# Linear attention: the products with the carried sum and the product of k and v issued as 32-column products, in one step with the products of the values

## Chip, core and metric

The kernel runs on one core of one Trainium2 chip. The metric is the device time of one execution in microseconds (us); the time before is the median of three executions. TensorE executes the matrix products, VectorE (DVE), ScalarE (ACT) and GpSimd (POOL) the elementwise work, and SyncE (SP) issues the DMA transfers. In the profile, PE is the row of matrix products of TensorE and PEld the row of its weight loads.

## What is computed

The program is a stack of four blocks over an input of 8 sequences, 1024 positions and 256 features, all in float32, each block with a layer norm in front and a residual around it: linear (flow) attention with its own feed-forward, a dense feed-forward, softmax attention, and a feed-forward with 4-bit quantized operands. The change lies in the first one:

```
q = sigmoid(heads(Wq)); k = sigmoid(heads(Wk)); v = heads(Wv)       # 16 heads of 16
...
vs = v * src_comp[..., None]
kv = cumsum(einsum('bhld,bhlm->bhldm', k, vs), axis=2)              # causal, per head 16 x 16
x  = einsum('bhld,bhldm->bhlm', qs, kv) * sink_alloc[..., None]
attn = x @ Wo + bo
```

The kernel computes the causal sum in chunks of 128 positions. For each chunk it adds two parts: the product of q with the sum of k times v over all earlier chunks of the sequence (the carried sum, called `kv_sum`), and the masked products of q and k inside the chunk times the values of the chunk.

## The kernel before

A sequence has 8 chunks of 128 positions, in two groups of four, so there are 64 chunks and 16 groups. A planner (class `Plan`) writes the program out: every piece of work is a generator that yields what it needs next (tiles, PSUM banks, a free slot), the planner keeps for each engine a modelled time at which it is free, and the part that can go first goes next (`run`, line 231). `took` (line 140) holds the modelled costs; for a matrix product it takes a quarter of the cost where the weights have at most 32 columns (line 158). All five engines are kept in exactly the order in which the instructions were issued (`PINNED`, line 38), and every instruction is issued through one helper, so that the profile shows one line, L268, for all of them and groups have to be told apart by the names of tiles. Since the order follows from the modelled costs and from the needs, an edit of one part moves the work of all others too.

The parts that run side by side are the linear attention (`linear_group`, `linear_chunk`), the two dense feed-forwards (`dense`, with `norms_1` and `norms_2`) and softmax attention with the quantized feed-forward (`soft_chunk`). PSUM has 8 banks, and a part asks for as many as it needs with `banks=`.

A chunk of linear attention (`linear_chunk`, line 897) goes through these steps:

- `bank<-wqkv,n0T` makes the values; DVE adds the bias and writes the scaled values into a padded tile `v_pad` (5 buffers), where each head has 32 columns, half of them zero.
- ACT writes `qz`, q split by even and odd heads, and TensorE makes the products of q and k in four groups of 32 rows (`bank<-qz,k`, line 951). DVE masks them into four tiles `sc` (line 963).
- TensorE turns k round (`bank<-ident,k`, line 973) and ACT copies it to SBUF as `kT`.
- The output bank: two products of full width with the carried sum (`bank<-q,kv_sum`, lines 980 to 990) and 16 products whose weights have 32 columns (`bank<-sc,v_pad`, lines 991 to 1001), all accumulated in the same bank. ACT copies the bank to `xo`.
- After that, as a need of its own that the planner may place later (line 1006): two products of full width of `kT` with the values (`bank<-v_pad,k`, lines 1008 to 1015). DVE multiplies them with the block diagonal `bdiag`, so that only the 16 x 16 block of each head stays (`kv`, line 1018), and POOL adds them to the carried sum (`kv_sum`, line 1028). The last chunk of a sequence leaves this step out, and the first one has no carried sum, so each is done 56 times.
- `bank<-w_L_attn_Wo,xo` is the output projection of the chunk.

The two products of k and v before:

```
yield pe(kT, banks=1)
kvbank = mm_bank()
for k in range(2):
    nc.tensor.matmul(kvbank[:, k * P : (k + 1) * P], lhsT=kT[:, k, :],
                     rhs=v_columns(pad, range(4 * k, 4 * k + 4)), start=True, stop=True)
```

`v_columns(pad, pairs)` (line 652) picks the nonzero columns of the given pairs of heads, 32 columns for a pair.

Of the kernel before, what the change touches and what calls it, by code (L numbers as in the profile page):

```python
# [13 lines left out]
ALU = mybir.AluOpType  # L14
AX = mybir.AxisListType

P = 128
D = 256
# [39 lines left out]
class Plan:  # L58
# [142 lines left out]
    def pe(self, *tiles, **kw):  # L201
        return self.need("tensor", tiles, **kw)

    def dve(self, *tiles, **kw):
        return self.need("vector", tiles, **kw)

    def act(self, *tiles, **kw):
        return self.need("scalar", tiles, **kw)
# [78 lines left out]
def block_stack_kernel(ctx: ExitStack, tc: tile.TileContext, a: dict, out: bass.AP):  # L287
# [20 lines left out]
    plan = Plan(tc, tc.nc)  # L308
    nc, pe, dve, act, dma = plan, plan.pe, plan.dve, plan.act, plan.dma
# [15 lines left out]
    def mm_bank():  # L325
        bank = ps.tile([P, 512], F32, tag="bank", name="bank")
        plan.bank(bank)
        return bank
# [4 lines left out]
    def fresh(kind, need, name=None):  # L333

        need.fresh = kind
        yield need
        return make(kind, name)

    def make(kind, name=None):
        bufs, width, dtype = TILES[kind]  # L340
        t = wk.tile([P, width], dtype, tag=kind, name=name or kind, bufs=bufs)
        plan.take(kind, t)
        return t
# [29 lines left out]
    bdiag = const.tile([P, P], F32, name="bdiag")  # L373
# [130 lines left out]
    def turned(srcs):  # L504

        bank = tr_bank()
        for i, src in enumerate(srcs):
            nc.tensor.transpose(bank[:, i, :], src, ident)
        return bank[:, : len(srcs), :]
# [4 lines left out]
    def two(t):  # L514
        return t.rearrange("p (k t) -> p k t", k=2)
# [136 lines left out]
    def v_columns(v, pairs):  # L652

        return bass.AP(
            tensor=v.tensor,
            offset=v.offset + 64 * pairs.start,
            ap=[list(v.ap[0]), [64, len(pairs)], [64 - DH, 2], [1, DH]],
        )
# [38 lines left out]
    def running(out, cur, carry, b, first, last):  # L697
# [16 lines left out]
    count = {  # L714
        "halves": 0,
        "dense": 0,
        "acc": 0,
        "res": 0,
        "v": 0,
        "scored": 0,  # L720
        "attended": 0,
        "linear": 0,
# [14 lines left out]
    def half_fits(p, kind, half):  # L737
        return half in groups[p][kind] or count["halves"] < HALVES
# [11 lines left out]
    def linear_group(p):  # L750
# [143 lines left out]
        for i in range(G):  # L894
            plan.start(linear_chunk(p, i, n0T, comp, qk), p + 0.55 + 0.03 * i)

    def linear_chunk(p, i, n0T, comp, qk):

        s, g = divmod(p, NG)
        past, c = seqs[s]["past"], p * G + i  # L900
        here = slice(i * P, (i + 1) * P)
        yield pe(n0T, banks=1, when=lambda: count["v"] == c and c - count["attended"] < V_PADS)
        bank = mm_bank()
        for k in range(2):
            nc.tensor.matmul(
                bank[:, :D],
                lhsT=n0T[:, k, here],
                rhs=wqkv[:, k, 2 * D :],
                start=k == 0,
                stop=k == 1,  # L910
            )
        count["v"] += 1
        pad = v_pads[c % V_PADS]
# [17 lines left out]
                when=lambda: groups[p].get("scaled")  # L931
# [13 lines left out]
        banks = []  # L945
        for r in range(4):
            rows = slice(32 * r, 32 * r + 32)
            bank = mm_bank()
            banks.append(bank)
            for k in range(2):  # L950
                nc.tensor.matmul(
                    bank[:, k * D : (k + 1) * D],
                    lhsT=qk[1][rows, k, here],
                    rhs=qz[rows, k, :, :],
                    start=True,
                    stop=True,
                )
        plan.drop(tile_qz)
        scores = []
# [10 lines left out]
        end = g == NG - 1 and i == G - 1  # L970
        if not end:
            yield pe(banks=1, at=p + 0.66 + 0.06 * i, when=lambda: count["attended"] == c)
            bank = turned([qk[1][:, k, here] for k in range(2)])
            kT = two((yield from fresh("lin", act(bank), "k")))
            nc.scalar.copy(kT, bank)
        kv = past.get("kv")
        yield pe(pad, *scores, *([] if kv is None else [kv]), banks=1, when=lambda: count["attended"] == c)
        kv = past.get("kv")

        bank = mm_bank()[:, :D]  # L980
        for k in range(2):
            if kv is not None:
                nc.tensor.matmul(
                    bank[:, k * P : (k + 1) * P],
                    lhsT=kv[:, k, :],
                    rhs=qk[0][:, k, here],
                    start=k == 0,
                    stop=False,
                    skip_group_check=True,
                )  # L990
        for k in range(2):
            for e in range(2):
                for r in range(4):
                    nc.tensor.matmul(
                        bank[32 * r : 32 * r + 32, k * P : (k + 1) * P],
                        lhsT=pad[:, 8 * k + 2 * r + e, :],
                        rhs=scores[r][:, 2 * k + e, :],
                        start=kv is None and k == 0 and e == 0,
                        stop=k == 1 and e == 1,
                        skip_group_check=True,  # L1000
                    )
        plan.drop(*scores)
        xo = two((yield from fresh("lin", act(bank), "xo")))
        nc.scalar.copy(xo, two(bank))
        if not end:
            yield pe(kT, banks=1)
            kvbank = mm_bank()
            for k in range(2):
                nc.tensor.matmul(
                    kvbank[:, k * P : (k + 1) * P],  # L1010
                    lhsT=kT[:, k, :],
                    rhs=v_columns(pad, range(4 * k, 4 * k + 4)),
                    start=True,
                    stop=True,
                )
            plan.drop(kT)
            new = two((yield from fresh("lin", dve(kvbank), "kv")))
            nc.vector.tensor_tensor(
                new,
                two(kvbank[:, :D]),  # L1020
                bdiag.unsqueeze(1).to_broadcast([P, 2, P]),
                ALU.mult,
            )
            total = past["kv"] = wk.tile([P, 2, P], F32, tag="kv_sum", name="kv_sum", bufs=2)
            if kv is None:
                nc.gpsimd.tensor_copy(total, new)
            else:
                nc.gpsimd.tensor_tensor(total, kv, new, ALU.add)
            plan.drop(new)
        count["attended"] += 1  # L1030
        yield pe(xo, banks=1, at=p + 0.7 + 0.06 * i)
        bank = mm_bank()
        for k in range(2):
# [12 lines left out]
            banks=1,  # L1046
            at=p + 0.74 + 0.06 * i,
            when=lambda: half_fits(p, "hT", i // 2) and count["dense"] >= p - 1,
# [358 lines left out]
```

## Time and profile before

| quantity | value |
| --- | --- |
| median of three executions | 2785.93 us (2783.41 to 2787.86) |
| the profiled execution, its own time | 2781.91 us |
| its span, from the first to the last instruction | 2780.2 us |
| mean granted clock of TensorE | 0.983 |
| PE busy | 2643.3 us, 95% |
| DVE busy | 1947.2 us, 70% |
| ACT busy | 1255.4 us, 45%, of it 402.9 us in 314 table loads |
| POOL busy | 557.4 us, 20% |

A float32 matrix product leaves two records on the PE row and two on the PEld row: the 112 products with the carried sum appear as x224. Records overlap, since the next one starts before the one before it has ended, so the length of a record (275 ns at the median of these 224) is not what it costs; the distance between the starts of two groups is. A form such as `128*32 128x128` gives the rows and columns of the weights and then the size of the moving operand. The numbers in front of the lines of a timeline are the start and the length of a group in microseconds.

### The profile page before, as it was taken

What the parts mean: (1) busy time and instruction counts of PE and PEld (TensorE: products, weight loads), DVE (VectorE), ACT (ScalarE), POOL (GpSimd) and SP (SyncE); (2) the same over time, 40 slices, a digit from 0 to 9 for tenths busy, and PEclk for the clock granted to TensorE, in tenths of its full rate; (3) what the DMA queues carried; (4) which work ended last, traced back from release to release, by engine and by line L of the source; (5) the groups of instructions that cost most, each with busy time, mean ns of one, the idle gap of its engine ahead of it and who ended that gap; (6) DMA issues with size and microseconds to landing.
All of it is one profiled execution on the core that took longest, in us unless ns stands there. A gap on an engine that the chain in (4) does not pass through costs nothing.

```text
span 2780.2 us, 42805 instructions
## 1 busy us (share of the span) xinstructions
PE 2643.3 (95%) x15276; PEld 2018.2 (73%) x15276; DVE 1947.2 (70%) x4403; ACT 1255.4 (45%) x2482; POOL 557.4 (20%) x1100
## 2 busy tenths in 40 slices
PE   3978999999999999999999999999999999999997
PEld 1767777777777777777777777777777777777665
DVE  6877686785867768586685867668586766846565
ACT  2424443545444463545535454354544445444242
POOL 1323222121221212122131222212122121211000
PEclk7989999999999999999999999999999999999998
DMA  3234231322323222231222323132232312222000
GB/s 106 79 95 132 79 101 61 92 65 73 97 63 95 69 74 73 80 103 59 82 70 75 93 73 93 52 99 65 72 92 67 100 57 83 70 72 84 19 12 14
DMA packets 283204, 211.43 MB, mean 76 GB/s; under 512 B 23921, under 2 KB 270705, under 8 KB 282993
## 3 DMA queue, kind: packets, MB, share of 16 engines
q1 hardware_dynamic: 282992, 208.71, 25.0%
q8 instruction: 122, 2.00, 0.3%
q14 instruction: 90, 0.73, 0.1%
HBM read 189.74 MB, written 18.87 MB: 75 GB/s over the span
## 4 chain that ended last, share of the span: by engine, by line
PE 75%; DVE 14%; DMA 5%; ACT 4%; issue 2%; POOL 1%; SPq 0%; DVEq 0%; ACTq 0%; POOLq 0%
PE bank L268 75%; DVE prod L268 4%; DMA spread<-packed 2%; DVE n L268 2%; ACT L268 1%; DVE hid L268 1%; DVE spread L268 1%; DMA w_ff<-in_L_ffn_w_dram 1%; DVE ln_st L268 1%; ACT q_c L268 1%; DVE x_amax L268 1%; DVE u L268 1%; DMA packed<-flow 1%; DVE div L268 1%; POOL ln_rstd L268 1%
## 5 line engine op out<-in xcount | busy, mean ns | idle before, releaser
L268 PE MATMUL bank<-half,w_ff 128*128 128x256 f32 x2048 | 534.6, 384 | 16.6 <-DMA w_ff<-in_L_ffn_w_dram 14.0
L268 PE MATMUL bank<-w_ff,hidden 128*128 128x256 f32 x2048 | 526.0, 382 | 0.0
L268 PEld LDWEIGHTS bank<-half,w_ff 128*128 128x128 f32 x2048 | 380.9, 192 | 87.5 <-issue 24.7
L268 ACT ACT_TABLE_LOAD x314 | 402.9, 1283 | 78.5 <-PE bank L268 69.8
L268 PEld LDWEIGHTS bank<-w_ff,hidden 128*128 128x128 f32 x2048 | 367.8, 191 | 66.5 <-issue 24.1
L268 POOL TENSOR_SCALAR ln_ve<-ln_mv 128x1 f32<-128x1 f32 x384 | 89.1, 232 | 1312.9 <-DVE ln_mv L268 1302.0
L268 ACT ACTIVATE hidden<-bank,c_L_ffn_b 128x256 f32<-128x256 f32 x256 | 121.1, 473 | 337.7 <-PE bank L268 337.2
L268 PE MATMUL bank<-n2T,qT 128*128 128x512 f32 x512 | 241.6, 595 | 1.0 <-ACT qT L268 1.0
L268 PE MATMUL bank<-vt,probT 128*128 128x256 f32 x1024 | 234.1, 382 | 2.1 <-DVE probT L268 2.1
L268 DVE TENSOR_TENSOR hid<-hid,bank 128x352 f32<-128x352 f32 x128 | 65.9, 515 | 240.5 <-PE bank L268 159.7
L268 POOL TENSOR_TENSOR ln_rstd<-ln_ve,neghalf 128x1 f32<-128x1 f32 x384 | 225.9, 588 | 32.0
L268 PEld LDWEIGHTS bank<-vt,probT 128*128 128x128 f32 x1024 | 194.9, 192 | 42.4 <-issue 11.7
L268 DVE TENSOR_TENSOR sc<-bank,triu 128x512 f32<-128x512 f32 x256 | 162.0, 682 | 52.1 <-PE bank L268 52.1
L268 PE MATMUL bank<-wdT,hqT 128*128 128x256 f32 (+1 forms) x768 | 193.5, 395 | 0.8 <-ACT hqT L268 0.8
L268 ACT ACTIVATE hidden<-bank,c_L_attn_b 128x256 f32<-128x256 f32 x256 | 121.4, 474 | 145.6 <-PE bank L268 144.1
L268 PE MATMUL bank<-wgT,xqT 128*128 128x352 f32 x512 | 177.0, 468 | 1.6 <-ACT xqT L268 1.5
L268 PE MATMUL bank<-wuT,xqT 128*128 128x352 f32 x512 | 173.4, 461 | 0.0
L268 PEld LDWEIGHTS bank<-wdT,hqT 128*128 128x128 f32 (+1 forms) x768 | 141.7, 193 | 42.1 <-issue 23.7
L268 POOL TENSOR_TENSOR xr<-xr,b_L_attn_ln_b 128x256 f32<-128x256 f32 x64 | 53.4, 852 | 491.1 <-DMA xr<-in_L_attn_inputs_dram 490.9
L268 PEld LDWEIGHTS bank<-n2T,qT 128*128 128x128 f32 x512 | 93.1, 190 | 72.3 <-issue 63.2
L268 PEld LDWEIGHTS bank<-wuT,xqT 128*128 128x128 f32 x512 | 98.0, 191 | 54.7 <-issue 1.0
L268 PEld LDWEIGHTS bank<-wgT,xqT 128*128 128x128 f32 x512 | 92.7, 190 | 47.5 <-issue 12.8
(174 smaller groups left out, 4377.5 us busy)
## 6 DMA issues: line engine op xcount, KB each, us to landing
w_ff<-in_L_attn_W_dram SPq DMA_DIRECT2D x512, 128.0 KB
w_ff<-in_L_ffn_w_dram SPq DMA_DIRECT2D x512, 128.0 KB
spread<-packed SPq DMA_DIRECT2D x96, 256.0 KB
x<-in_L_attn_inputs_dram SPq DMA_DIRECT2D x64, 128.0 KB
xr<-in_L_attn_inputs_dram SPq DMA_DIRECT2D x64, 128.0 KB
rows<-res SPq DMA_DIRECT2D x64, 128.0 KB
rows<-rows SPq DMA_DIRECT2D x64, 128.0 KB
out_dram<-y SPq DMA_DIRECT2D x64, 128.0 KB
```

Source lines behind the costliest of these rows:

```text
L268: ins = method(*args, **kw)
```

## The change

Three things are done.

1. The two full-width products with the carried sum become eight products with 32 columns of weights each; each of the four that belong together writes other 32 partitions of the bank. They stay in the same place, ahead of the 16 products of the values.
2. The two full-width products of k and v become eight products with 32 columns of weights and 32 moving columns, and follow the products of the values at once; the need of their own is gone, so `kT` and a second bank are needed ahead of the whole step, and the copy to `xo` is issued after them.
3. The bank of k and v now holds only 64 columns, 32 for each half. DVE spreads each half over four groups of 32 columns while it multiplies with `bdiag`: two operations of 128 columns in place of one of 256.

The diff, cut to its core:

```diff
         kv = past.get("kv")
-        yield pe(pad, *scores, *([] if kv is None else [kv]), banks=1, when=lambda: count["attended"] == c)
+        yield pe(
+            pad,
+            *scores,
+            *([] if kv is None else [kv]),
+            *([] if end else [kT]),
+            banks=2,
+            when=lambda: count["attended"] == c,
+        )
...
         for k in range(2):
-            if kv is not None:
-                nc.tensor.matmul(
-                    bank[:, k * P : (k + 1) * P],
-                    lhsT=kv[:, k, :],
-                    rhs=qk[0][:, k, here],
+            for r in range(4):
+                if kv is not None:
+                    nc.tensor.matmul(
+                        bank[32 * r : 32 * r + 32, k * P : (k + 1) * P],
+                        lhsT=kv[:, k, 32 * r : 32 * r + 32],
+                        rhs=qk[0][:, k, here],
...
         plan.drop(*scores)
+        if not end:
+
+            kvbank = mm_bank()[:, :64].rearrange("p (k d) -> p k d", k=2)
+            for k in range(2):
+                for r in range(4):
+                    nc.tensor.matmul(
+                        kvbank[32 * r : 32 * r + 32, k, :],
+                        lhsT=kT[:, k, 32 * r : 32 * r + 32],
+                        rhs=v_columns(pad, range(4 * k + r, 4 * k + r + 1)),
+                        start=k == 0,
+                        stop=True,
+                        skip_group_check=True,
+                    )
+            plan.drop(kT)
         xo = two((yield from fresh("lin", act(bank), "xo")))
         nc.scalar.copy(xo, two(bank))
         if not end:
-            yield pe(kT, banks=1)
-            kvbank = mm_bank()
+            new = two((yield from fresh("lin", dve(kvbank), "kv")))
             for k in range(2):
-                nc.tensor.matmul(
-                    kvbank[:, k * P : (k + 1) * P],
-                    lhsT=kT[:, k, :],
-                    rhs=v_columns(pad, range(4 * k, 4 * k + 4)),
-                    start=True,
-                    stop=True,
+                nc.vector.tensor_tensor(
+                    new[:, k, :].rearrange("p (r d) -> p r d", r=4),
+                    kvbank[:, k, :].unsqueeze(1).to_broadcast([P, 4, 32]),
+                    bdiag.rearrange("p (r d) -> p r d", r=4),
+                    ALU.mult,
                 )
-            plan.drop(kT)
-            new = two((yield from fresh("lin", dve(kvbank), "kv")))
-            nc.vector.tensor_tensor(
-                new,
-                two(kvbank[:, :D]),
-                bdiag.unsqueeze(1).to_broadcast([P, 2, P]),
-                ALU.mult,
-            )
```

More of the change, by code (lines that the diff above doesn't have):

```diff
@@ L981, in linear_chunk @@
         for k in range(2):
-            if kv is not None:
-                nc.tensor.matmul(
-                    bank[:, k * P : (k + 1) * P],
-                    lhsT=kv[:, k, :],
-                    rhs=qk[0][:, k, here],
-                    start=k == 0,
-                    stop=False,
-                    skip_group_check=True,
-                )
+            for r in range(4):
[5 more added lines that the diff above has]
+                        start=k == 0,
+                        stop=False,
+                        skip_group_check=True,
+                    )
         for k in range(2):
@@ L1002, in linear_chunk @@
         plan.drop(*scores)
+        if not end:
[6 more added lines that the diff above has]
+                        rhs=v_columns(pad, range(4 * k + r, 4 * k + r + 1)),
+                        start=k == 0,
+                        stop=True,
+                        skip_group_check=True,
+                    )
+            plan.drop(kT)
         xo = two((yield from fresh("lin", act(bank), "xo")))
@@ L1005, in linear_chunk @@
         if not end:
-            yield pe(kT, banks=1)
-            kvbank = mm_bank()
+            new = two((yield from fresh("lin", dve(kvbank), "kv")))
             for k in range(2):
-                nc.tensor.matmul(
-                    kvbank[:, k * P : (k + 1) * P],
-                    lhsT=kT[:, k, :],
-                    rhs=v_columns(pad, range(4 * k, 4 * k + 4)),
-                    start=True,
-                    stop=True,
-                )
-            plan.drop(kT)
-            new = two((yield from fresh("lin", dve(kvbank), "kv")))
-            nc.vector.tensor_tensor(
-                new,
-                two(kvbank[:, :D]),
-                bdiag.unsqueeze(1).to_broadcast([P, 2, P]),
-                ALU.mult,
-            )
+                nc.vector.tensor_tensor(
[3 more added lines that the diff above has]
+                    ALU.mult,
+                )
             total = past["kv"] = wk.tile([P, 2, P], F32, tag="kv_sum", name="kv_sum", bufs=2)
```

## The prediction

> **What bounds the kernel now.** I read the page first, then busy time by stretches, then the PE groups by form, then timelines of PE around one chunk.
>
> ```profile
> PE 2643.3 (95%) x15276; PEld 2018.2 (73%) x15276; DVE 1947.2 (70%) x4403; ACT 1255.4 (45%) x2482; POOL 557.4 (20%) x1100
> PE 75%; DVE 14%; DMA 5%; ACT 4%; issue 2%; POOL 1%; SPq 0%; DVEq 0%; ACTq 0%; POOLq 0%
> ...
> 0.00:100.00 100.00, 46.27 (x377) 32.04 (x381) 67.26 (x170) 23.84 (x59) 17.67 (x46) 0.81 0.29 82
> 100.00:400.00 300.00, 269.83 (x1681) 211.27 (x1672) 218.02 (x492) 121.01 (x257) 82.55 (x150) 0.94 0.34 102
> 400.00:2400.00 2000.00, 1971.39 (x11539) 1513.40 (x11538) 1435.08 (x3218) 963.17 (x1859) 418.19 (x822) 1.00 0.26 79
> 2400.00:2780.00 380.00, 355.81 (x1693) 261.46 (x1691) 226.86 (x526) 147.39 (x308) 39.04 (x83) 0.97 0.13 40
> ```
>
> The second line is the chain that ended last; the rows of stretches give bounds, length, then PE, PEld, DVE, ACT and POOL busy, clock, DMA share, GB/s. From 400 to 2400 us PE is idle for 28.6 us in all: it is the bound there, and a microsecond of TensorE time saved is one off the span. Before 400 us it is idle for 83.9 us, waiting for data.
>
> The groups concerned, by form, and one chunk in order of time:
>
> ```profile
> L268 PE MATMUL bank<-sc,v_pad 128*32 128x128 f32 x2048 | 69.7, 276 | 0.2 <-DVE sc L268 0.2
> L268 PE MATMUL bank<-q,kv_sum 128*128 128x128 f32 x224 | 35.5, 281 | 0.0
> L268 PE MATMUL bank<-v_pad,k 128*128 128x128 f32 x224 | 35.2, 280 | 0.0
> ...
> 93.61 0.44 PE L268 MATMUL bank<-ident,k 128*128 128x128 f32 x2
> 93.88 0.61 PE L268 MATMUL bank<-q,kv_sum 128*128 128x128 f32 x4
> 94.42 1.08 PE L268 MATMUL bank<-sc,v_pad 128*32 128x128 f32 x32
> 95.43 0.71 PE L268 MATMUL bank<-v_pad,k 128*128 128x128 f32 x4
> ...
> 94.42 0.43 PE L268 MATMUL bank<-sc,v_pad 128*32 128x128 f32 x8
> 94.42 0.54 PE L268 MATMUL bank<-sc,v_pad 128*32 128x128 f32 x12
> ```
>
> The distances between starts are what counts. The last two lines are the same group cut by narrow windows: four more records lengthen it by 0.11 us. So 32-column records start in sets of four, about 0.109 us a set (32 records are 8 sets, 0.87 of the 1.01 us), and a full-width record of 128 moving columns takes the same 0.11 us alone. Four 32-column products thus cost what one full-width product costs.
>
> ```profile
> 2239.05 1.45 PE L268 MATMUL bank<-wgT,xqT 128*128 128x352 f32 x4
> 2240.34 1.35 PE L268 MATMUL bank<-wuT,xqT 128*128 128x352 f32 x4
> 2241.52 0.61 PE L268 MATMUL bank<-v_pad,k 128*128 128x128 f32 x4
> 2241.97 0.60 PE L268 MATMUL bank<-ident,prob 128*128 128x128 f32 x4
> ...
> 165.12 0.28 PE L268 MATMUL bank<-total,front 128*128 128x1 f32 x2
> 165.26 0.36 PE L268 MATMUL bank<-total,same 128*128 128x1 f32 x2
> ```
>
> In the steady part the product of k and v costs 2241.97 - 2241.52 = 0.45 us. The group at 2239.05 follows 32-column products and takes 1.29 us, the like one after it 1.18: leaving the narrow mode costs the first full-width group 0.11 us, on top of the 0.10 us gap inside the 0.54 of the carried sum (4 x 0.11 = 0.44).
>
> **What the Trainium skill says.** "TensorE: Matmul & The Clock Gate", section "The mechanism" (Part 3): products whose outputs lie in different groups of 32 partitions run at the same time in the array, each about 4 ns after the one before. The trace agrees in kind: a set of four in 0.109 us, and the window from 94.42 to 94.45 us holds the starts of all four records of a set, so they are at most 10 ns apart. "TensorEngine Tiling (Array Packing)", "Key Properties": a change of the tiling mode drains TensorE; the trace shows it at 0.10 us in and about 0.2 us out. The same page, "Instruction Overhead": a product with one moving column takes as long as one with 60 (some 60 cycles each), so one shouldn't take the factor from a small dimension. This bears on the 32 moving columns; the trace has no such form, and its two records of one moving column (165.12 to 165.26, 0.14 us) are full width and so say little of narrow weights. Prices from the first page: "LDWEIGHTS (loading the stationary operand)" gives columns / 1.2 ns, an estimate of 27 ns for 32 columns, and the section on the gap "Wait — 56ns, not 53.3ns?" a floor of 25 ns from start to start.
>
> **The change part by part.**
>
> *Carried sum, 56 chunks.* Four full-width records (0.44 us) become 16 narrow ones, four sets of 0.109 us (0.436). Nothing gained. The narrow mode starts earlier, so the drain moves in front of it.
>
> *Product of k and v, 56 chunks.* Out go 0.45 us. In come 16 records in four sets, with 32 moving columns, a quarter of the 128 that take 0.109 us: 0.027 us of streaming a set. The weights of a set load beside the set before, estimated at 27 ns. Bounds: four records a set at 7 ns each give 0.11 us in all; 25 ns for each record one after another give 0.40; sets that don't get shorter with the moving operand 0.44. I take 0.035 us a set, 0.14 us in all, since streaming and loading both come out near 0.03 and the trace shows four records starting together. Saving 0.31 us x 56 = 17.4 us, from 18.8 at the lower bound to 0.6 at the upper.
>
> *Changes of mode.* Counted in the compiled order of both programs, changes between full width, 32 columns and 32 rows go from 302 to 294, and all eight that go are returns to full width. At 0.1 us of drain and 0.1 us of load each: -1.6 us.
>
> *DVE.* One operation of 0.414 us becomes two of 128 columns. The nearest row is the 128-column product from PSUM, 0.270 us (16 of them, 4.3 us, in the groups by form). 2 x 0.270 - 0.414 = +0.126 us, +7.1 us over 56. DVE is busy 1435 of 2000 us in the steady part, so PE's work hides it; without that cover it is 7 us.
>
> *The wait.* The step now asks for `kT` and two banks before its first product. Queued behind it on PE are the other parts' products, but the planner only emits the step when its model has both ready, and the turn of k stays ahead of it in the compiled order. `xo` is issued after the k-v products but needs only the first bank. I take nothing; bounds -0.05 and +0.1 us a chunk (-3 to +6 us).
>
> *ACT and SP.* The new order has 286 table loads instead of 315 in the old one; 29 x 1.283 us is 37 us less on an engine at 45%: hidden behind PE. On SP, the `w_ff` loads around the first spreads move: in the new order one more pair stands before the four spread transfers that held SP at 141 us. PE waited 14 us for `w_ff` of the second feed-forward, nearly all of it before 400 us.
>
> *Given back early.* Seven of the 56 chunks run before about 210 us, ahead of stalls of 7 us for weights whose time the transfers set. Their 7 x 0.31 = 2.2 us are taken as lost there.
>
> Sum: -17.4 - 1.6 + 2.2 = -16.8 us. Against the profiled execution's own 2781.91 us that is 2765. The median shown stands 4.0 us above that execution; so 2769 us for a median, -0.6%.
>
> **Rivals.**
>
> *The k-v products stay at the issue floor* (0.40 to 0.44 us). For it: the skill's warning on small dimensions. Against it: four starts within 0.03 us in this trace. Saved are then 2.8 to 0.6 us, and 1.6 for the modes, less the early part: 2782 to 2785, no change that can be told.
>
> *The new order has fewer stalls as well.* For it: 28.6 us idle in the steady part, 13.3 of them waits for `prob` from ACT, which loses 37 us of table loads, and the 14 us for `w_ff`. Against it: nothing in the change aims at these. Half of both stalls gone, -14: about 2755 us.
>
> *The carried sum comes late: slower.* It is made by two DVE operations instead of one, then POOL (0.73 us), and the next chunk's step waits for it. In the new order two chunks of a group follow each other with only a feed-forward product, the output projection, the turn of k and another feed-forward product between them: 0.86 + 0.86 + 0.22 + 0.86 = 2.8 us. The chain needs 0.27 + 0.54 + 0.73 = 1.5 us and DVE's queue: two mask operations (0.68 each) in front would nearly fill the gap, four would leave 1.4 us of PE idle. Before, PE never waited for `kv_sum`, and POOL is at 20%; in the new DVE order I find the `kv` operations ahead of the next chunk's masks. It decides from (16.8 + 5.6) / 56 = 0.40 us a chunk on; at 0.7 us the time is 2769 + 39 = 2808.
>
> **How the numbers follow.** A measurement of this kernel tells about 0.2% (5.6 us) from no change: faster is below 2780.4, slower above 2791.5. Forecast 2769 (2760 to 2778), chance 0.61; fewer stalls 0.16; issue floor 0.14; late sum, or another stall that the new order makes, 0.09. Faster: the first two and a little of the third, 0.79. Same: the rest of the third, 0.12. Slower 0.09. The range leaves out the last case and the ends of the others: 2754 to 2786.
>
> **What would show it.** In the changed profile the k-v group `32x32` x16 should span about 0.14 us from its start to the end of starting, the carried sum 0.44; PE busy should fall by some 17 us with idle about the same between 400 us and the end of the dense part; DVE busy should rise by 7; nobody should wait for `kv_sum`. If PE busy falls and the time doesn't, look for PE waits behind `kv_sum`, `sc` or `w_ff`. I am wrong if a set with 32 moving columns takes 0.1 us, or if the new order idles PE.

## The result, and the profile after

The changed kernel takes 2753.12 us (median, 2750.45 to 2756.59); the kernel before 2786.89 us beside it. The ratio is 0.988, 95% interval 0.9861 to 0.9898: 33.8 us less, twice the 16.8 us of the forecast and just below the low end of the range (2754 us). The profiled execution took 2750.45 us, with a span of 2748.6.

Busy time of each engine, and the shares of the chain of work that ended last, from the page of the changed kernel:

```profile
PE 2614.9 (95%) x16620; PEld 1998.1 (73%) x16620; DVE 1953.3 (71%) x4459; ACT 1219.6 (44%) x2453; POOL 597.7 (22%) x1100
PE 83%; DVE 11%; DMA 2%; ACT 2%; issue 1%; POOL 1%; SPq 0%; DVEq 0%; POOLq 0%; ACTq 0%
```

The busy time by stretches of the same execution (bounds, length, then PE, PEld, DVE, ACT and POOL busy, clock, DMA share, GB/s):

```profile
0.00:100.00 100.00, 44.80 (x441) 30.54 (x445) 66.90 (x168) 22.36 (x58) 16.98 (x43) 0.81 0.31 83
100.00:400.00 300.00, 268.66 (x1889) 212.02 (x1882) 223.73 (x510) 122.20 (x263) 85.02 (x154) 0.95 0.36 106
400.00:2400.00 2000.00, 1988.48 (x12953) 1526.71 (x12951) 1467.39 (x3330) 936.05 (x1858) 461.75 (x838) 1.00 0.26 79
2400.00:2780.00 380.00, 312.93 (x1348) 228.87 (x1348) 195.25 (x453) 139.00 (x276) 33.92 (x68) 0.98 0.12 37
```

Two things are to be seen. PE is busy for 28.4 us less in all. And in the steady part (400 to 2400 us) its idle time fell from 28.6 to 11.5 us. But behind 2400 us, up to the end of the span, it rose from 24.4 to 35.7 us, and before 400 us from 83.9 to 86.5, so that over the whole execution PE is idle for 133.7 us where it was 136.9. Of the 31.6 us by which the span of the profiled execution shrank, 28.4 are thus busy time and 3.2 idle time, and the busy time alone fell by more than the 19 us that the prediction had for the products and the changes of mode. Busy time is not all work, though: a record of 128 columns is some 275 ns long and the next one can start 110 ns after it, so a short wait disappears inside the record before it.

One chunk in the steady part of the changed kernel, in order of time on PE (start, busy, and after the shapes the number of records):

```profile
1260.57 1.03 PE L268 MATMUL bank<-wv,n2T 128*128 128x256 f32 x4
1261.53 0.65 PE L268 MATMUL bank<-q,kv_sum 128*32 128x128 f32 x16
1261.99 1.06 PE L268 MATMUL bank<-sc,v_pad 128*32 128x128 f32 x32
1262.86 0.31 PE L268 MATMUL bank<-v_pad,k 128*32 128x32 f32 x16
1263.10 1.13 PE L268 MATMUL bank<-w_ff,hidden 128*128 128x256 f32 x4
1264.07 0.59 PE L268 MATMUL bank<-w_L_attn_Wo,xo 128*128 128x256 f32 x2
```

From start to start the carried sum takes 0.46 us (before, with the drain behind it, 0.54), the values 0.87 (before, with the way out, 1.01), the product of k and v with the way out 0.24 (before 0.45 alone). The drain now lies in the group ahead (0.96 instead of 0.86) and the load of full-width weights still in the group behind (0.97 instead of 0.86). A chunk thus goes from 0.54 + 1.01 + 0.45 = 2.00 to 0.10 + 0.46 + 0.87 + 0.24 = 1.67 us: 0.33 us, x 56 = 18.5.

The same view of the product of k and v alone, in a window cut at 1262.95 us:

```profile
1262.86 0.28 PE L268 MATMUL bank<-v_pad,k 128*32 128x32 f32 x12
```

12 of its 16 records have started within 0.09 us, so a set of four records with 32 moving columns takes about 0.03 us.

Where PE waited in the steady part of the kernel before (what it waited for: us in total, times, longest):

```profile
PE bank L268 <- ACT prob L268: 13.3, 18, 1.3
PE bank L268 <- DVE sc L268: 5.6, 7, 0.9
PE bank L268 <- DVE prod L268: 5.5, 6, 1.2
```

And in the changed kernel:

```profile
PE bank L268 <- DVE u L268: 3.7, 6, 0.6
PE bank L268 <- ACT hidden L268: 3.4, 6, 0.6
PE bank L268 <- ACT half L268: 2.8, 6, 0.5
PE bank L268 <- DVE n L268: 1.3, 3, 0.5
```

None of these waits touches the products that were changed. Behind 2400 us the largest waits are, before and then in the changed kernel:

```profile
PE bank L268 <- DVE hid L268: 6.1, 4, 2.3
PE bank L268 <- ACT prob L268: 5.0, 3, 3.8
```

```profile
PE bank L268 <- DVE hid L268: 14.4, 5, 7.3
PE bank L268 <- ACT prob L268: 10.4, 8, 3.8
```

So a part of the waiting moved to the end. The largest wait of the steady part, for `prob`, can be followed at one place on ACT in the kernel before:

```profile
1148.56 1.28 ACT L268 ACT_TABLE_LOAD   x1 [0.54 <-PE bank L268]
1149.86 0.47 ACT L268 ACTIVATE hidden<-bank,c_L_attn_b 128x256 f32<-128x256 f32 x1
1150.35 1.28 ACT L268 ACT_TABLE_LOAD   x1
1151.64 0.69 ACT L268 ACTIVATE prob<-bank,nmax 128x512 f32<-128x512 f32 x1
```

Two table loads of 1.28 us stand ahead of the exponential, with one activation of the feed-forward between them, and PE waits 0.72 us until it can turn `prob` round (at 1152.47 us). The new order places these parts differently: no wait for `prob` is left in the steady part, while over the whole execution those waits fall only from 18.3 to 14.5 us. Which of both causes, the products or the order, made how much was the first question for the chip.

### The profile page after: what moved, and what is told of

Same layout as the page of the kernel before. It is cut to its first block, busy times and chain, and to the rows that moved or that the text cites. A ratio compares the mean times of both kernels' runs of the same rounds, so it can differ in the third digit from the quotient of the medians.

```text
span 2748.6 us, 45646 instructions
## 1 busy us (share of the span) xinstructions
PE 2614.9 (95%) x16620; PEld 1998.1 (73%) x16620; DVE 1953.3 (71%) x4459; ACT 1219.6 (44%) x2453; POOL 597.7 (22%) x1100
## 4 chain that ended last, share of the span: by engine, by line
PE 83%; DVE 11%; DMA 2%; ACT 2%; issue 1%; POOL 1%; SPq 0%; DVEq 0%; POOLq 0%; ACTq 0%
PE bank L268 83%; DVE hid L268 3%; DVE n L268 1%; DVE x_amax L268 1%; DVE ln_st L268 1%; DMA spread<-packed 1%; DVE mx L268 1%; DVE sc L268 1%; DVE prod L268 1%; ACT L268 1%; DMA w_ff<-in_L_ffn_w_dram 1%; SPq L268 0%; DVE u L268 0%; DVE x_r L268 0%; POOL ln_rstd L268 0%
## 5 line engine op out<-in xcount | busy, mean ns | idle before, releaser
L268 PE MATMUL bank<-half,w_ff 128*128 128x256 f32 x2048 | 533.8, 384 | 17.1 <-DMA w_ff<-in_L_ffn_w_dram 13.7
L268 POOL TENSOR_SCALAR ln_ve<-ln_mv 128x1 f32<-128x1 f32 x384 | 102.4, 267 | 1110.1 <-DVE ln_mv L268 1099.6
L268 POOL TENSOR_TENSOR ln_rstd<-ln_ve,neghalf 128x1 f32<-128x1 f32 x384 | 237.4, 618 | 32.0
L268 POOL TENSOR_TENSOR xr<-xr,b_L_attn_ln_b 128x256 f32<-128x256 f32 x64 | 62.6, 996 | 531.3 <-DMA xr<-in_L_attn_inputs_dram 531.1
L268 ACT ACTIVATE hid<-bank 128x352 f32<-128x352 f32 x128 | 59.3, 463 | 154.0 <-PE bank L268 152.6
```

Source lines behind the costliest of these rows:

```text
L268: ins = method(*args, **kw)
```

## The experiments

In all of them the reference is the kernel before, timed beside them; ratios are of the runs with their 95% intervals. e5 to e8 and e11 have the order that the planner makes by itself. In e1 to e4, e9 and e10 the planner does not choose: the parts that it had picked, 8872 picks in the kernel before ("old" in the table) or 8816 in the changed one ("new"), were written down and are played back, so that every engine's instructions keep their order whatever the edit does to the modelled costs (in the traces of e1 to e4 and e10, PE's records of all other products come in the same sequence as in the kernel whose order is played):

```diff
     def run(self):
-        while self.parts:
-            now = self.free.get("tensor", 0.0)
...
+        for n in np.frombuffer(zlib.decompress(base64.b85decode(ORDER)), np.uint16):
+            next(self.parts[n], None)
```

The helper's line is L256 or L257 in these kernels. The changed kernel itself was timed only once, with the first result, and the experiments on three later occasions, on which the median of the kernel before lay between 2785.49 and 2788.94 us. Differences to the changed kernel are therefore good to some 3 us at best.

| kernel | order | median us | ratio to the kernel before |
| --- | --- | --- | --- |
| changed kernel | new | 2753.12 | 0.988 (0.9861 to 0.9898) |
| e1: narrow products | old | 2764.81 | 0.9923 (0.9907 to 0.9939) |
| e2: full-width products | new | 2774.05 | 0.9957 (0.9941 to 0.9974) |
| e3: only k-v narrow, in its own place | old | 2781.93 | 0.9985 (0.9978 to 0.9992) |
| e4: only the carried sum full-width | new | 2759.26 | 0.9903 (0.9889 to 0.9917) |
| e5: full width, model's k-v price a quarter | own | 2800.79 | 1.0044 (1.0027 to 1.0061) |
| e6: full width, joined step | own | 2805.94 | 1.0061 (1.0046 to 1.0076) |
| e7: kernel before, model's latency 0.25 | own | 2806.47 | 1.0062 (1.0047 to 1.0077) |
| e8: changed kernel, model's DVE price 0.18 | own | 2792.88 | 1.0016 (1.0007 to 1.0026) |
| e9: no 64-row products | new | 2735.36 | 0.9819 (0.9802 to 0.9836) |
| e10: DVE operations twice | new | 2759.89 | 0.9904 (0.9887 to 0.9921) |
| e11: model prices changes of mode | own | 2768.39 | 0.9936 (0.9918 to 0.9954) |

### Products and order taken apart (e1, e2)

e1 has the three edits of the change, but the products of k and v are issued at the end of the step of the values while the part still stops where it stopped before, so that its picks match those of the kernel before:

```diff
         plan.drop(*scores)
+        if not end:
+            kvbank = mm_bank()[:, :64].rearrange("p (k d) -> p k d", k=2)
...
         if not end:
             yield pe(kT, banks=1)
-            kvbank = mm_bank()
```

> The narrow products of the change, in one step with the products of the values, with all other instructions of every engine in exactly the order of the kernel before. Theory A (the cheap products make all of the gain, the new order none): the full gain, about 2753 us. Theory B (the products save some 20 us of TensorE time, the rest of the 34 us comes from fewer waits in the new order): 2765 to 2769 us, PE busy down by 18 to 22 us, and in the steady part (400 to 2400 us) PE still idle for about 28 us with the waits for prob from ACT still there.

e2 is the changed kernel with full-width products in the same places; each of the two DVE operations takes its 128 columns of the bank as they are. The carried sum goes back to its two full-width products too. The edit for k and v, against the changed kernel:

```diff
-            kvbank = mm_bank()[:, :64].rearrange("p (k d) -> p k d", k=2)
+            kvbank = mm_bank()[:, :D]
             for k in range(2):
-                for r in range(4):
...
+                nc.tensor.matmul(kvbank[:, k * P : (k + 1) * P], lhsT=kT[:, k, :],
+                    rhs=v_columns(pad, range(4 * k, 4 * k + 4)), start=True, stop=True)
```

> The order of the changed kernel on every engine, but both pairs of products in full width, in the same places, and the two DVE operations kept. Theory A: no gain is left, about 2787 us. Theory B: the order keeps its own part, 12 to 15 us: 2771 to 2775 us, PE idle in the steady part about 12 us as in the changed kernel.

Measured: 2764.81 us for the narrow products in the old order, 2774.05 us for the full-width ones in the new order. Theory B holds, and the parts add: 21.0 us from the products, 11.7 us from the order, 32.7 together against 33.8 for the whole change. The steady rows of e1 and then of e2:

```profile
400.00:2400.00 2000.00, 1970.83 (x12720) 1509.71 (x12719) 1441.40 (x3273) 967.75 (x1865) 417.93 (x825) 1.00 0.26 79
```

```profile
400.00:2400.00 2000.00, 1989.24 (x11701) 1526.54 (x11700) 1454.38 (x3292) 927.30 (x1838) 459.08 (x829) 1.00 0.26 79
```

With the old order PE is idle for 29.2 us there although the products are cheap (13.3 of them for `prob`, as before), with the new one for 10.8 although they are not. In the steady part the idle time goes with the order. The end goes the other way: behind 2400 us PE is idle for 26.3 us in e1 and for 35.5 in e2.

Over the whole execution the split into busy and idle time is less clean. The narrow products save 19.3 us of busy time in the old order (2643.3 to 2624.0) and 27.4 in the new one (2642.3 to 2614.9). An estimate that doesn't hang on that split takes, in each of the four traces, the time of PE from its first record to its last, less the usual distance to the next start for every record (for 128, 256, 352 and 512 columns 0.110, 0.216, 0.296 and 0.429 us; for a set of four narrow ones 0.109, or 0.029 with 32 columns, and 0.218 with 32 rows; 0.06 for 64 columns or fewer). The products themselves then differ by 18.1 us. What is left over, waits and changes of mode together, is 259.5 us before, 257.6 in e1, 249.8 in e2 and 246.0 in the changed kernel. So the new order is worth 10 to 12 us with either kind of product: 16 to 22 us less are lost in the steady part, and 9 us more behind 2400 us. The 2 to 4 us that the narrow products save on top of their own 18.1 fit the changes of mode, which they lower from 302 to 292 in the old order and from 311 to 294 in the new one, at about 0.2 us each.

### What the parts of the change are worth (e3, e4, e10)

e3 makes only the product of k and v narrow and leaves it where it was (`yield pe(kT, banks=1)` stays in front of it, the carried sum keeps its two full-width products).

> The kernel before, in its own order, with only the product of k and v made narrow, left in its own later place among full-width products, and two DVE operations. If the price of the products is all that counts: 56 x 0.31 = 17 us less, 2769 us. If each change of the array's mode costs 0.1 us in and 0.1 to 0.2 us out, the change back and forth takes the saving away: 2783 to 2789 us.

Measured: a ratio of 0.9985, 3.9 us of medians, close to the 2783 to 2789 us that were expected if the changes of mode take the saving away (2781.93). The cheap product alone, put between full-width ones, is worth a fifth of the 21.0 us that it saves in e1 together with the narrow sum, next to the values. PE of e3 in order of time:

```profile
1577.54 1.35 PE L256 MATMUL bank<-wuT,xqT 128*128 128x352 f32 x4
1578.82 0.33 PE L256 MATMUL bank<-v_pad,k 128*32 128x32 f32 x16
1579.08 0.66 PE L256 MATMUL bank<-ident,prob 128*128 128x128 f32 x4
```

The group ahead takes 1.28 us where the like takes 1.18, the product itself 0.26 with the way out, and a full group behind a narrow one 0.05 to 0.10 us more than elsewhere: nearly all of the 0.45 us of the full-width product is paid again. In all, the changes of mode rise from 302 to 400. The joining pays, because it needs no change of mode of its own.

e4 is the changed kernel with the carried sum back in two full-width products.

> The changed kernel in its own order with the product of the carried sum back in full width. By the price of the products alone (0.44 us against 0.44) nothing changes: 2753 us. With changes of mode counted, the 16 of 56 that follow the 32-row products pay another way out and in, about 0.2 us each: 2755 to 2758 us.

Measured: 2759.26 us. Its interval overlaps the changed kernel's (0.9889 to 0.9917 against 0.9861 to 0.9898), so the time alone leaves it open, and it lies a little above the 2755 to 2758 us that were expected with changes of mode. The profile has a part of it: returns to full width in the order of instructions rise from 135 to 151, since 16 of the 56 sums now follow the 32-row products of q and k directly. Such a sum and the values behind it take 1.54 us from start to start in e4 where the narrow sum and the values take 1.33, which makes 3.3 us for the 16; behind full-width products the two kinds cost the same within 0.01 us, the way into the narrow mode included. The group of the sum itself is busy for 35.8 us against 36.1. What narrowing the sum gains thus comes from the changes of mode and not from the products; the other 3 us of the 6.1 between the medians, and why PE is busy for 11.5 us more (2626.4 instead of 2614.9), are not explained.

e10 issues each DVE operation on the k-v bank twice, to see whether what the change adds on DVE is hidden.

```diff
             for k in range(2):
+              for _ in range(2):
                 nc.vector.tensor_tensor(
                     new[:, k, :].rearrange("p (r d) -> p r d", r=4),
```

> The changed kernel in its own order with each of the 112 DVE operations on the k-v bank issued twice, with the same result: 112 x 0.28 = 31 us more on DVE, four operations in place of two between the k-v products and the carried sum. If PE hides what the change added on DVE: 2751 to 2757 us, and nobody waits for kv_sum. If the longer chain to the carried sum shows: 56 x 0.56 = 31 us at most, 2760 to 2785 us.

Measured: 2759.89 us, 6.8 us above the changed kernel, with intervals that overlap, and between the two forecasts. Of 31 us more on DVE about a fifth may show. No product waits for the carried sum, and one weight load does, for 0.3 us; what grows is the wait for `u`, from 3.7 to 7.6 us in the steady part. So the 6.1 us that the change itself adds on DVE (1947.2 to 1953.3) are probably nearly hidden: by the same share they would be worth one or two microseconds.

### Is the better order a part of the change, or a draw (e5, e6, e7, e8, e11)

The new order came out of the planner's model, which saw three things: a cheaper product, a step fewer, and a different DVE price. e5 gives the model the cheaper product alone and leaves the instructions of the kernel before:

```diff
+            if op == "matmul" and "v_pad" in kw["rhs"].tensor.name:
+                cost *= 0.25
```

> The kernel before with its full-width products; only the planner's model prices the two k-v products at a quarter, so that only the order changes. If the new order is better because the model sees these products as cheap: about 2774 us, as with the order of the changed kernel. If the gain of the order is chance, any value between 2770 and 2792 us; if it comes from the joined step alone: 2786 us.

e6 has the joined step alone, with full-width products and one DVE operation.

> Full-width products, priced as before, but the k-v products joined to the step of the values as in the change, with one DVE operation; the planner makes its own order. If joining the step makes the order better: 2772 to 2778 us. Joining full-width products to narrow ones adds 14 returns to full width (157 instead of 143), about 3 us. If the gain of the order is chance, any value between 2770 and 2792 us.

e7 and e8 change nothing but a number in the model that has nothing to do with the change: `after = 0.25` instead of 0.2 for TensorE in the kernel before, and `cost = 0.18 + each * size` instead of 0.15 for DVE in the changed kernel.

> The kernel before with the same instructions; only the planner's modelled latency after a matrix product is 0.25 instead of 0.2, so that the order changes for a reason that has nothing to do with the change. If orders differ by chance, the time moves by up to 12 us either way: 2774 to 2798 us. If an order is worth what its edit does for the work, it stays at 2783 to 2789 us.

> The changed kernel with the same instructions; only the planner's fixed price of a DVE operation is 0.18 instead of 0.15. If the 12 us of the new order were chance, another order gives some of them back: 2752 to 2768 us. If they belong to the narrow step, they stay: 2750 to 2756 us.

e11 tells the model of the changes of mode that the traces show:

```diff
+        if queue == "tensor":
+            shape = (128, 128) if op == "transpose" else kw["lhsT"].shape
+            mode = min(shape[0], 128) <= 32, shape[-1] <= 32
+            if mode != getattr(self, "mode", mode):
+                cost += 0.12 if any(mode) else 0.2
+            self.mode = mode
```

> The changed kernel with the same instructions; the planner's model adds 0.12 us for a change into a narrow mode and 0.2 us for a return to full width, so that only the order changes. If orders get better with a truer model: below 2750 us. If the order of the changed kernel is a lucky draw: 2755 to 2800 us.

Measured: 2800.79, 2805.94 and 2806.47 us where the products are those of the kernel before (its own: 2789 beside them), and 2792.88 and 2768.39 us where they are those of the changed kernel. e5 to e7 are 12 to 18 us slower than the kernel before beside them; e8 and e11 are 40 and 15 us slower than the changed kernel. In e5 to e8 that is more spread than the expectations had allowed. Neither the cheaper price nor the joined step makes a better order by itself, since each alone made a worse one (both together with full-width products were not tried), and in e7 and e8 a number that has nothing to do with the change moves the time by 18 and by 40 us. A model that prices the changes of mode (e11) made no better order either. As far as these draws show, the 11.7 us are a property of this one order, not of the edits taken one by one. Both kernels also have the fastest order that the planner made for their products here, out of four for full width and three for narrow ones; whether the numbers of its model had been chosen for that is not known.

The steady row of e8, with the same instructions as the changed kernel, and its largest waits:

```profile
400.00:2400.00 2000.00, 1962.01 (x12616) 1501.90 (x12618) 1448.40 (x3264) 916.58 (x1822) 438.61 (x822) 1.00 0.26 79
```

```profile
PE bank L268 <- ACT prob L268: 11.2, 15, 1.5
PE bank L268 <- DVE hid L268: 7.2, 6, 1.8
PE bank L268 <- DVE v L268: 6.2, 8, 1.5
```

PE is idle for 38.0 us where the changed kernel has it idle for 11.5. Table loads don't tell the orders apart: e8 has 274 in its order and e5 275, fewer than the 286 of the changed kernel. Nor does the longest stretch of the chain of work in which PE waited for nothing: it is 294.1 us in the changed kernel and 151.0 in e8, but 77.9 in e1, which is 28 us faster than e8 with the same products. Why the planner's greedy choice falls into one order or the other was not settled; with orders this sensitive I don't take one more run as an explanation.

### The price of a mode, tried elsewhere (e9)

If it is the change of mode that costs, a gain of this kind can be had at another place. The down projection of the last feed-forward ends in a product of 64 rows, since 704 is five and a half times 128. e9 lets that product take the last 128 columns of `hid`, with zero weights for the 64 that the tile ahead of it holds already (the loading of these weights and the turn of `hid` change with it, not shown):

```diff
+DOWN_TILES = INTER_TILES[:-1] + [(INTER - P, P)]
...
+    tc.nc.gpsimd.memset(wdT[: P // 2, len(INTER_TILES) - 1, :], 0.0)
...
-        for k, (f0, rows_) in enumerate(INTER_TILES):
+        for k, (f0, rows_) in enumerate(DOWN_TILES):
             nc.tensor.matmul(
```

> The changed kernel in its own order; in the last feed-forward the product of 64 rows at the end of the down projection becomes one of 128 rows (columns 576 to 703 of hid, with zero weights for the 64 that the tile before it already holds), so that the array keeps its full mode there. In the traces the group of 12 records with this product takes 2.88 us where 12 full ones take 12 x 0.216 = 2.59. If a change of mode is what costs, 64 x 0.29 = 18 us go: 2731 to 2739 us. If short products cost by themselves and not by the change of mode: 2750 to 2756 us.

Measured: 2735.36 us, 17.8 us below the changed kernel, where 18 were expected from the trace. The product now has 128 rows, half of them zero, and takes less time. The group and the one behind it in the changed kernel and then in e9:

```profile
1274.27 2.95 PE L268 MATMUL bank<-wdT,hqT 128*128 128x256 f32 x12
1277.15 0.44 PE L268 MATMUL bank<-ident,h 128*128 128x128 f32 x2
```

```profile
1269.43 2.75 PE L257 MATMUL bank<-wdT,hqT 128*128 128x256 f32 x12
1272.02 0.38 PE L257 MATMUL bank<-ident,h 128*128 128x128 f32 x2
```

From start to start 2.88 us became 2.59. The turn of the last part of `hid`, which also grows from 64 to 128 columns, makes no difference: its group takes 0.22 us in both kernels. e9 by itself can't tell a change of mode from a short product that is dear in its own right, since it takes both away. The starts of single records in the changed kernel speak for the change of mode: full-width records of the group start 0.216 us apart, the last of them and the first short one 0.309, the two short ones 0.320, the second short one and the next group 0.306. Full-width groups next to 32-column ones show the same: the last full-width record ahead stands 0.309 before the first narrow one, and in the full-width group behind the first two records stand 0.320 apart and the others 0.216. So the longer distances come with the last record of a mode and the first of the next, short or not. This kernel is faster than both that were compared, with a ratio of 0.9819 (0.9802 to 0.9836) to the kernel before.

## Why the prediction was off

- **PE bounds the steady part, and a microsecond saved there is one off the span:** right. e1, in the order of the kernel before, saves 19.3 us of PE busy time, 17.6 us of the profiled span and 21.0 us of the medians.
- **Product of k and v, 0.14 us:** right. Four sets at about 0.03 us and the way out make 0.24 us, and the way out was paid behind the values before. The floor of one start per 25 ns that a rival took from the Trainium skill doesn't hold for records that write four different groups of 32 partitions: "TensorE: Matmul & The Clock Gate", section "The mechanism", draws about 4 ns between the starts of products in different tiles of the array, the trace of before showed them at most 10 ns apart, and this kernel starts 12 in 0.09 us.
- **Carried sum, nothing gained:** right for the products (36.1 us busy against 35.5). The gain of 1.6 us from changes of mode was the right kind of term, but its count (302 to 294) mixes the edits with the new order: at a fixed order the narrow products take away 10 or 17 changes, an estimated 2 to 4 us. e4 puts narrowing the sum at some microseconds through them, without separating it well.
- **Given back early, +2.2 us:** not borne out in the old order: in e1 the first product of `total` in the fourth group starts at 395.4 us where it started at 400.0, so the early saving was kept there. In the changed kernel PE is idle before 400 us for 86.5 us where it was 83.9, which is of the size of the term, but the order is another one there, so this stays open.
- **DVE hidden:** right within what e10 can tell.
- **The wait for kT and two banks, and the later copy to xo, nothing:** right. In the changed kernel `xo` costs PE 0.8 us in all.
- **The carried sum comes late:** didn't happen; no product waits for `kv_sum`, and even in e10 only one weight load does, for 0.3 us.
- **The new order.** This is the step that failed. The sum has no term for it: "I take nothing" was said of the waits that the edits add, and PE's idle time was to stay about the same in the steady part. It fell there from 28.6 to 11.5 us, and e2, which has the new order without the narrow products, is 11.7 us faster than the kernel before. The rival "the new order has fewer stalls as well" named the right kind of cause, with a chance of 0.16. That its 14 us lie close to the 11.7 is luck: they were half of the waits for `prob` in the steady part and of those for `w_ff`, but the waits for `w_ff` before 400 us stayed at 13.7 us, and those for `prob`, gone from the steady part, came back in part elsewhere. The range's low end was that rival's time, which took the given-back 2.2 us along, so the sum of both parts fell just outside.

The size of the failed term could not have been had from the edits: e5 to e8 and e11 show that the planner's orders differ by up to 40 us for the same instructions. What could be had, by letting the planner's model vary a little, was its spread, and with it a wider range on both sides. The chances given to a gain (0.16) and to a loss (0.09) by the order were too low for orders that differ so much.

## What to carry to other kernels

Count changes between array shapes as instructions of their own: here each way into narrow products and back cost about 0.3 us together, so a cheap product of another shape was worth its full saving only beside others of its shape, and padding a short product with zeros to the shape of its neighbours can be faster than leaving it short. Where a planner with modelled costs makes the order, any edit is two changes, the edit and a new order. Play the old order back under the new instructions, and the new order under the old ones, before either is credited; then keep the better order on its own merits.

## What was not expected of the hardware

A product with half of its rows zero took less time in its place than the short one (2.59 against 2.88 us for the group); the distances between starts put this down to the change of mode that it avoids. Four records with 32 columns of weights and 32 moving columns took about 0.03 us together, a quarter of the 0.109 us with 128 moving columns, so that neither the number of instructions nor the loads of weights set a floor at this size.
